# Silu gates of sequence groups 2 to 4: computed during the first group's scan and reloaded from device memory

## The chip, the cores and the metric

One Trainium2 chip, one of its cores. The metric is the device time of one execution in microseconds (us), median over runs. The profile is of one further execution. The engines are PE (matrix products, with its weight loads shown as PEld), DVE (vector), ACT (activation functions), POOL (general) and SP, which here only issues DMAs.

## The reference, cut to what matters

There are 32 sequences of 256 tokens and 256 channels. A state-space block runs first, then two attention and feed-forward layers. The change touches the first block only:

```python
xr, gate = jnp.split(x @ W_in.T, 2, axis=-1)          # 512 + 512 channels
xr = xr + t_emb[:, None, :]
xc = silu(causal_conv4(xr))                            # 4 taps per channel
xn = layernorm(xc)
# Bm, Cm, dt from xn;  Ad, Bd from dt, Bm
h  = clip(h * Ad + Bd * xn_t, -10, 10)                 # one step per token, in order
y  = Cm . h  + D * xn
out = (y * silu(gate)) @ W_out.T                       # 512 -> 256 channels
# then two layers: local attention, feed-forward
```

The gate half of `x @ W_in.T` needs only the input `x`. It does not depend on the scan, and it is used only after a step's `y` is known.

## The kernel before

**Groups, chunks and slots.** The sequences are worked in four groups of eight (`GB = 8`, groups g = 0 to 3 in the code, 1 to 4 in words). A group's scan has 256 steps, one per token for its eight sequences at once, in eight chunks of 32 (`CH`, `NCH`). `group_scan(g)` writes an agenda: a dictionary from slot to the calls to be made there, filled by `at(slot, function, ...)`. One slot is one scan step, `s0` is the slot of a chunk's first step. `scan_slots` walks the agendas of all groups in order of slots. A scheduler then fixes each engine's order, near to this one; each engine runs its own list strictly in that order, and so does each DMA queue.

**Two stages.** The scan of group 1 has no attention beside it: slots run up to 274 (`S + DRAIN`) before the first attention product. I call it the first stage. After it, attention and feed-forward of group g run interleaved with the scan of group g + 1: 16 pairs of sequence and layer for each group, while the scan makes 8 chunks. Attention of group 4 runs with no scan beside it (the last stage).

**One step** (`step`, L716): DVE makes the new state `h` of 128 x 512 from the old one and a row `xrep`. The row comes from device memory by one SP DMA (`load_rows`, six slots ahead, six buffers) and is scaled on ACT (`scale_row`, L706). In the first stage two rows of every eight are made on PE instead (`spread_rows`, tile `bx`, L693). There are eight buffers for `h`; PE reads four steps of `h` at a time into `y` (`read_out`, L728), one product for each of four blocks of 32 array columns.

**Projection in the first stage.** For group 1, `project` (L399, tile `ps_in`) makes the four convolution channel blocks and the four gate blocks of each chunk from a loaded slice of x (`load_x`, tile `xg`). Beside that, units `u` make ahead the convolution half of groups 2 to 4: `ahead_load` (x slice `xa`, by SP), `ahead_project` (four matrix products 128x256, tile `ps_a`, L426), `ahead_copy` (one ACT copy of 128x512, L437) and `ahead_put` (one SP DMA of 256 KB to device memory). There are 48 units, two for each of 24 chunks, one at every 5.33 slots from slot -30 on. `load_projected` brings them back.

**The gate in groups 2 to 4.** At each chunk `load_x` brings the x slice again (two SP DMAs of 128 KB at slot s0 + 6), `project` makes the four gate blocks at slots s0 + 13 to 18 (eight matrix products; the profile shows each as two records), `gate_th` copies each block in another order to `sg` (ACT, helper `reorder`, L371) and takes a Tanh (ACT, L768), and `gate_out` makes twice the Silu from them (DVE, L773). The factor of two is taken out of `w_out_sb`, halved once by `halve` (POOL, L331). In group 1 `gate_th` uses Silu at once, and `copy_y` (L819) puts the factor of two back. `out_gate` (L799) multiplies by `sg`, 9 slots into the next chunk for the second half; `sg` has one buffer.

Of the kernel before, what the change touches and what calls it, by code (L numbers as in the profile page):

```python
# [10 lines left out]
FP = mybir.dt.float32  # L11
BF = mybir.dt.bfloat16
I32 = mybir.dt.int32
AF = mybir.ActivationFunctionType
ALU = mybir.AluOpType
# [4 lines left out]
P = 128  # L20
# [4 lines left out]
NC_ = DI // P  # L25
NS = 16
GB = 8
CH = 32
NCH = S // CH
# [44 lines left out]
def kernel(  # L74
# [29 lines left out]
    nc = tc.nc  # L104
    B = xT.shape[2]
    L = wqkv.shape[1]
    NG = B // GB
# [55 lines left out]
    for j in range(NJ):  # L163
# [18 lines left out]
        out=mask_t[:, 0:W], in_=mask_t[:, 0:W], compare_op=ALU.is_ge, fill=MASKED_LOW,  # L182
# [39 lines left out]
    def program(ctx, exact):  # L222
# [14 lines left out]
        def constants(at):  # L237
# [86 lines left out]
                ):  # L324
                    nc.scalar.dma_start(out=t, in_=src)

            def halve():


                tc.keep_in_program_order(  # L330
                    nc.gpsimd.tensor_scalar_mul(w_out_sb, w_out_sb, 0.5)  # L331
                )

            def load_tables():

                tab, sc = work("swp", "tab", 3), work("swp", "qk_sc", 3)
# [24 lines left out]
            at(-14, sums_w)  # L361
            at(-19, decay_rate)
            at(-16, load_later)
            at(14, halve)
            at(30, load_tables)
            for n in range(2 * L):
                at(50 + 6 * n, tables, n // L, n % L)
# [1 line left out]
        def reorder(out, ps, func):  # L369

            nc.scalar.activation(  # L371
                out.rearrange("p (q i b) -> p b i q", q=NQ, b=GB),
                ps.rearrange("p (b i q) -> p b i q", q=NQ, b=GB),
                func,
            )

        def group_scan(g):
# [8 lines left out]
            alone = g == 0  # L386
# [5 lines left out]
            def at(s, what, *args):  # L392
                agendas[-1].setdefault(s, []).append(partial(what, *args))
# [14 lines left out]


            def ahead_load(u):  # L410
                if u % 2 == 0:
                    gg, c = 1 + u // 2 // NCH, u // 2 % NCH
                    t = ap_.tile([P, KM, GB, CH], FP, tag="rot", name="xa", bufs=4)
                    for k in range(KM):
                        nc.sync.dma_start(
                            out=t[:, k],
                            in_=xT[:, k, gg * GB : (gg + 1) * GB, c * CH : (c + 1) * CH],
                        )
                    state["xa", u // 2] = t

            def ahead_project(u):
                ps = bank(ps_w, "w", "ps_a").rearrange("p (r n) -> p r n", r=2)
                for r in range(2):
                    ch = 2 * (u % 2) + r
                    for k in range(KM):
                        nc.tensor.matmul(  # L426
                            ps[:, r],
                            w_in_sb[:, k, ch * P : (ch + 1) * P],
                            state["xa", u // 2][:, k],
                            start=(k == 0),  # L430
                            stop=(k == KM - 1),
                        )
                state["pa", u] = ps

            def ahead_copy(u):
                t = aw.tile([P, 2, GB * CH], FP, tag="pT", name="xs_a", bufs=6)
                nc.scalar.copy(t, state.pop(("pa", u)))  # L437
                state["ta", u] = t

            def ahead_put(u):  # L440
# [3 lines left out]

            def load_projected(c, i):
                t = sp.tile([P, 2, GB * CH], FP, tag="xg", name="xp", bufs=2)
                nc.sync.dma_start(out=t, in_=projected[((g - 1) * NCH + c) * 2 + i])
                for r in range(2):
                    ck[c]["ps", 2 * i + r] = t[:, r]


            def load_x(c):
                xg = sp.tile([P, KM, GB, CH], FP, tag="xg", name="xg", bufs=2)
# [306 lines left out]
            def gate_th(c, ch):  # L760
                if ch == 0:
                    ck[c]["sg"] = sp.tile([P, NC_, GB * CH], FP, tag="sg", name="sg")
                sg = ck[c]["sg"][:, ch]
                reorder(sg, ck[c].pop(("ps", NC_ + ch)), AF.Silu if alone else AF.Copy)
                if alone:
                    return
                th = sp.tile([P, GB * CH], FP, tag="th", name="th_g", bufs=2)
                nc.scalar.activation(th, sg, AF.Tanh, scale=0.5)  # L768
                ck[c]["th_g", ch] = th

            def gate_out(c, ch):
                sg = ck[c]["sg"][:, ch]
                nc.vector.scalar_tensor_tensor(  # L773
                    sg, ck[c].pop(("th_g", ch)), 1.0, sg, ALU.add, ALU.mult
                )

            def gated(c, hb):

# [38 lines left out]
            def copy_y(c, d):  # L817
                yo = sp.tile([P, GB, CH], FP, tag="yo", name="yo", bufs=2)
                nc.scalar.activation(  # L819
                    yo.rearrange("p b (i q) -> p q i b", q=NQ),  # L820
                    ck[c].pop(("po", d))[:, 0 : GB * CH].rearrange(
                        "p (q i b) -> p q i b", q=NQ, b=GB
                    ),
                    AF.Copy,
                    scale=2.0 if alone else 1.0,
                )
                ck[c]["yo", d] = yo

# [27 lines left out]
            for c in range(NCH):  # L856
                s0 = c * CH
                for hb in range(CH // TB):
                    s = s0 + hb * TB
                    for i in range(NI):  # L860
                        at(s + 4 * i + 5, read_out, c, hb, i)
                    at(s + 21, gated, c, hb)
                    at(s + 25, out_gate, c, hb)
                    at(s + 11, skip, c, hb)
                for ch in range(NC_):
                    at(s0 - 38 + 2 * ch, conv_in, c, ch)
                    at(s0 - 37 + 2 * ch, conv_taps, c, ch)
                    at(s0 - 36 + 2 * ch, conv_th, c, ch)
                    if not alone:
                        at(s0 - 35 + 2 * ch, conv_out, c, ch)  # L870
                for ch, s in enumerate((13, 16, 17, 18)):
                    at(s0 + s + 2, gate_th, c, ch)
                    if not alone:
                        at(s0 + s + 4, gate_out, c, ch)
                at(s0 - 25, raw_copy, c)
                at(s0 - 24, raw_turn, c)
                for j in range(NJ):
                    s = s0 - 26 + 4 * j
                    at(s + 2, norm_stats, c, j)
                    at(s + 5, norm_shift, c, j)  # L880
                    at(s + 5, norm_apply, c, j)
                    at(s + 6, norm_affine, c, j)
                    at(s + 9, norm_out, c, j)
                at(s0 - 11, length, c)
                at(s0 - 9, figures, c)
                at(s0 - 7, figures_in, c)
                at(s0 - 6, decay_th, c)
                at(s0 - 5, decays, c)
                at(s0 - 4, put_c, c, 0)
                at(s0 + 4, put_c, c, 1)  # L890
                for d in range(KM):
                    at(s0 + 45 + 2 * d, copy_y, c, d)
                    at(s0 + 46 + 2 * d, put_y, c, d)
            agendas.append({})
            for c in range(NCH):
                s0 = c * CH
                at(s0 - 43 if alone else s0 + 6, load_x, c)
                if alone:
                    for ch in range(NC_):
                        at(s0 - 40 + 2 * ch, project, c, ch)  # L900
                else:
                    for i in range(2):
                        at(s0 - 44 + 2 * i, load_projected, c, i)
                for ch, s in enumerate((13, 16, 17, 18)):
                    at(s0 + s, project, c, NC_ + ch)
                at(s0 - 27, raw_sums, c)
                for j in range(NJ):
                    at(s0 - 26 + 4 * j, norm_turn, c, j)
                at(s0 - 8, figures_out, c)
                for t in range(CH):  # L910
                    if not by_tensor(t):
                        at(s0 + t - 6, load_rows, c, t)
                    if by_tensor(t) and t % XR == 0:
                        at(s0 + t - 4, spread_rows, c, t)
                    at(s0 + t - 2, scale_row, c, t)
                for hb in range(CH // TB):
                    s = s0 + hb * TB
                    at(s - 9 if alone else s + 7, load_skip, c, hb)
                    at(s + 23, out_turn, c)
                for d in range(KM):  # L920
                    at(s0 + 43 + 2 * d, project_y, c, d)

            if alone:
                n = (NG - 1) * NCH * 2
                for u in range(n):
                    s = -30 + u * (NCH * CH) // n
                    at(s - 5, ahead_load, u)
                    at(s, ahead_project, u)
                    at(s + 2, ahead_copy, u)
                    at(s + 4, ahead_put, u)  # L930
# [731 lines left out]
```

## Time and profile before

| What | us |
|---|---|
| median of three runs | 3590.94 |
| lowest, highest of these | 3585.17, 3603.19 |
| the profiled execution's own time | 3582.75 |
| its span (first to last instruction) | 3581.0 |

| Engine | busy us | share of the span |
|---|---|---|
| PE | 3446.0 | 96% |
| PEld | 2253.9 | 63% |
| DVE | 2667.3 | 74% |
| ACT | 1998.7 | 56% |
| POOL | 1892.2 | 53% |

Busy time is the time covered by an engine's records. PE's records overlap and their ends are modelled, so PE is busy also where it could have taken more; what a product really takes is seen better in the time from one start to the next in a dense stretch. "x" counts records. Idle time is put down to what released the engine. The span holds the first stage (to about 460 us), the interleaved stage (to about 2800 us), and the last stage.

### The profile page before, as it was taken

Reading aid. Unit: us, or ns where it says so; the run is one execution under the profiler, and the core shown is the slowest. Engines: PE = TensorE matmul, PEld = TensorE weight load, DVE = VectorE, ACT = ScalarE, POOL = GpSimd, SP = SyncE. Lnnn points to the kernel's source line nnn. Section 1 sums busy time; section 2 is a strip of 40 time slices with the busy share of each in tenths; the row PEclk is TensorE's granted clock in tenths of the full one; section 3 lists DMA queues with packets and bytes.
Section 4 is the critical chain, followed back from the end, with each engine's and each line's share of the span. In section 5 each row is a group of like instructions: output and inputs, shape, how many; then the busy total and the mean of one; then the engine's idle time right before and its main releaser. Section 6 shows DMA issues by size and latency. Waiting matters only on the chain.

```text
span 3581.0 us, 57673 instructions
## 1 busy us (share of the span) xinstructions
PE 3446.0 (96%) x20220; PEld 2253.9 (63%) x20220; DVE 2667.3 (74%) x5049; ACT 1998.7 (56%) x3599; POOL 1892.2 (53%) x1842
## 2 busy tenths in 40 slices
PE   7999989999999999999999999999999999999999
PEld 4555335666656666666666666666666677777777
DVE  5888889888788777888787778888877555555553
ACT  4666656656555665566566655655666444434442
POOL 4433477645556555655565556555544454544551
PEclk9999999999999999999999999999999999999999
DMA  7887665445354545444454555534454112011101
GB/s 207 219 221 213 198 174 149 120 117 143 109 144 125 149 141 148 130 118 127 118 142 125 138 149 140 143 106 131 114 141 122 54 50 61 13 30 38 33 27 37
DMA packets 468767, 435.68 MB, mean 122 GB/s; under 512 B 228723, under 2 KB 308084, under 8 KB 468340
## 3 DMA queue, kind: packets, MB, share of 16 engines
q1 hardware_dynamic: 384018, 419.88, 42.0%
q10 hardware_dynamic: 84450, 12.01, 2.0%
q8 instruction: 163, 2.67, 0.3%
q14 instruction: 136, 1.11, 0.1%
HBM read 383.54 MB, written 46.66 MB: 120 GB/s over the span
## 4 chain that ended last, share of the span: by engine, by line
PE 61%; DVE 19%; DMA 7%; POOL 6%; ACT 4%; issue 3%; SPq 0%; ACTq 0%; DVEq 0%; POOLq 0%
PE ps_qkv L989 13%; PE pa L1375 13%; DVE h L716 7%; PE po_f L1402 7%; DMA xrep<-xnd 5%; PE ps_wo L1039 5%; PE y L728 4%; PE ov L1271 4%; PE sc L1215 3%; PE ps_out L808 3%; PE ps_in L399 2%; PE tr_qk L1028 2%; PE rs L1252 2%; ACT xrep L706 2%; DVE acc L489 2%
## 5 line engine op out<-in xcount | busy, mean ns | idle before, releaser
L716 DVE CUSTOM_DVE_ANT_0 h<-h,xrep,lim 128x512 f32<-128x512 f32 x1024 | 961.0, 938 | 228.9 <-ACT xrep L706 196.6
L706 ACT ACTIVATE xrep<-xrep,beta 128x512 f32<-128x512 f32 x960 | 672.3, 718 | 341.4 <-DMA xrep<-xnd 219.8
L989 PE MATMUL ps_qkv<-qkv,res 128*128 128x512 f32 x1536 | 713.5, 601 | 17.9 <-DVE rinv L1260 8.4
L1375 PE MATMUL pa<-hT,w 128*128 128x256 f32 (+1 forms) x2816 | 675.1, 382 | 11.3 <-DVE zT L799 10.7
L1375 PEld LDWEIGHTS pa<-hT,w 128*128 128x128 f32 (+1 forms) x2816 | 516.9, 188 | 152.9 <-issue 35.4
L1013 POOL TENSOR_TENSOR rot<-rot,swp 128x512 f32<-128x512 f32 x256 | 339.9, 1328 | 475.3 <-DVE swp L1010 423.5
L1021 POOL TENSOR_TENSOR rn<-ss,neg_half 128x8 f32<-128x8 f32 x256 | 466.8, 1823 | 18.4 <-DVE ss L1019 7.8
L989 PEld LDWEIGHTS ps_qkv<-qkv,res 128*128 128x128 f32 x1536 | 282.2, 191 | 301.6 <-issue 241.4
L728 PE MATMUL y<-h,ly 128*32 128x512 f32 x2048 | 348.9, 609 | 16.9 <-DVE h L716 13.9
L1327 POOL TENSOR_TENSOR rstd<-ve,neg_half 128x2 f32<-128x2 f32 x64 | 46.9, 733 | 527.6 <-DVE ve L1325 511.3
L1393 DVE SCALAR_TENSOR_TENSOR ag<-pa,b_sb,ag 128x256 f32<-128x256 f32 x320 | 151.6, 474 | 222.4 <-ACT ag L1386 222.3
L1402 PE MATMUL po_f<-ag,w 128*128 128x256 f32 x1280 | 309.0, 389 | 5.9 <-DVE fo L1413 3.8
L1022 POOL TENSOR_TENSOR rot<-rot,rn 128x512 f32<-128x512 f32 x256 | 289.4, 1130 | 20.0
L1402 PEld LDWEIGHTS po_f<-ag,w 128*128 128x128 f32 x1280 | 236.8, 191 | 71.3 <-issue 12.0
L1386 ACT ACTIVATE ag<-pa,b_sb 128x256 f32<-128x256 f32 x320 | 150.2, 469 | 233.1 <-PE pa L1375 232.1
L1002 ACT ACTIVATE sq<-ps_qkv 128x512 f32<-128x512 f32 x256 | 150.8, 595 | 185.1 <-PE ps_qkv L989 119.4
L1039 PE MATMUL ps_wo<-oT,wo 128*128 128x256 f32 x1024 | 231.7, 379 | 0.5 <-DVE ag L1393 0.5
L489 DVE SCALAR_TENSOR_TENSOR acc<-xr,wc_sb,acc 128x256 f32<-128x256 f32 x384 | 195.1, 531 | 47.7 <-POOL acc L478 47.2
L1005 DVE TENSOR_TENSOR rot<-ps_qkv,rc_sb 128x512 f32<-128x512 f32 x256 | 174.8, 683 | 65.6 <-ACT sq L1002 65.0
L1039 PEld LDWEIGHTS ps_wo<-oT,wo 128*128 128x128 f32 x1024 | 194.4, 190 | 28.1 <-DVE ag L1393 0.9
L1227 ACT ACTIVATE pT<-sc 128x512 f32<-128x512 f32 x384 | 202.3, 603 | 7.6 <-PE sc L1215 5.8
L1271 PE MATMUL ov<-pT,v_sb 128*64 128x256 f32 (+1 forms) x2048 | 183.7, 330 | 19.4 <-DVE ag L1393 19.3
(160 smaller groups left out, 5482.8 us busy)
## 6 DMA issues: line engine op xcount, KB each, us to landing
xrep<-xnd SPq DMA_DIRECT2D x960, 256.0 KB
rb<-inv SPq DMA_DIRECT2D x128, 256.0 KB
xnd<-xn SPq DMA_DIRECT2D x64, 256.0 KB
qkv<-in_wqkv_dram SPq DMA_DIRECT2D x24, 512.0 KB
ahead<-xs_a SPq DMA_DIRECT2D x48, 256.0 KB
xp<-ahead SPq DMA_DIRECT2D x48, 256.0 KB
xd<-xnd SPq DMA_DIRECT2D x192, 64.0 KB
w<-in_w_dram SPq DMA_DIRECT2D x80, 128.0 KB
```

The source lines that it names most:

```text
L489: nc.vector.scalar_tensor_tensor(acc, xr[:, :, k : k + CH], wc_sb[:, ch, k : k + 1], acc, ALU.mult, ALU.add,)
L706: scaled = nc.scalar.activation(bx, ck[c].pop(("bx", t), bx), AF.Copy, scale=ck[c]["beta"][:, t : t + 1])
L716: nc.vector._custom_dve(TENSOR_ADD_SAT, out=h_new, in0=state["h"], in1=bx, s0=ck[c]["lim"][:, 0, t : t + 1], s1=ck[c]["lim"][:, 1, t : t + 1],
L728: nc.tensor.matmul(ck[c]["y", hb][32 * q : 32 * q + 32, :], ly[hb % 2][:, 32 * t : 32 * t + 32], ck[c].pop(("h", hb * TB + t)), start=(i = ...
L989: nc.tensor.matmul(ps, res[b][:, k, t0 : t0 + W], wt["qkv", a][:, k], start=(k == 0), stop=(k == KM - 1),)
L1013: nc.gpsimd.tensor_add(rot, rot, swp)
L1021: nc.gpsimd.tensor_tensor(rn, ss, neg_half, ALU.pow)
L1022: nc.gpsimd.tensor_mul(rot, rot, bc(rn, 2, DH))
L1039: nc.tensor.matmul(po[:, d], wt["wo", 0][:, c, d * P : (d + 1) * P], oT[:, c, :], start=(c == 0), stop=(c == NC_ - 1),)
L1271: nc.tensor.matmul(ov[r * DH : (r + 1) * DH, i, kw * W :], self.qkv[b][2][:, kw, h * DH : (h + 1) * DH], self.p.pop((b, kw, i0 + i, r)), s ...
L1375: nc.tensor.matmul(dst[x], wt["w1", m][:, k, x], self.h[:, k], start=(k == 0), stop=(k == KM - 1),)
L1402: nc.tensor.matmul(self.po[:, d], wt["w2", 0][:, m, d * P : (d + 1) * P], self.ag[m], start=(m == 0), stop=(m == len(MCH) - 1),)
```

## The change

The units of the first stage now make all eight channel blocks of a chunk, not four: 96 units, four for each chunk, on one x slice each as before. Units 0 and 1 of a chunk are copied, units 2 and 3 (the gate) get two ACT instructions with Silu, in the order that `out_gate` reads. Each unit's result is put to device memory. The units start at slot -14 and not -30, and stand 2.875 slots apart. In groups 2 to 4, `load_x`, `project`, the Tanh and `gate_out` are gone; `load_gates` brings a chunk's four gate blocks back with two SP DMAs of 256 KB at slot s0 + 15. With no doubled gate left, `halve` and the scale in `copy_y` go.

```diff
-            def halve():
-                tc.keep_in_program_order(
-                    nc.gpsimd.tensor_scalar_mul(w_out_sb, w_out_sb, 0.5)
-                )
...
             def ahead_load(u):
-                if u % 2 == 0:
-                    gg, c = 1 + u // 2 // NCH, u // 2 % NCH
+                if u % 4 == 0:
+                    gg, c = 1 + u // 4 // NCH, u // 4 % NCH
...
             def ahead_project(u):
-                    ch = 2 * (u % 2) + r
+                    ch = 2 * (u % 4) + r
...
             def ahead_copy(u):
                 t = aw.tile([P, 2, GB * CH], FP, tag="pT", name="xs_a", bufs=6)
-                nc.scalar.copy(t, state.pop(("pa", u)))
+                ps = state.pop(("pa", u))
+                if u % 4 < 2:
+                    nc.scalar.copy(t, ps)
+                else:
+                    for r in range(2):
+                        reorder(t[:, r], ps[:, r], AF.Silu)
...
+            def load_gates(c):
+                sg = ck[c]["sg"] = sp.tile([P, NC_, GB * CH], FP, tag="sg", name="sg")
+                for i in range(2):
+                    nc.sync.dma_start(
+                        out=sg[:, 2 * i : 2 * i + 2],
+                        in_=projected[((g - 1) * NCH + c) * 4 + 2 + i],
+                    )
...
-                reorder(sg, ck[c].pop(("ps", NC_ + ch)), AF.Silu if alone else AF.Copy)
-                if alone:
-                    return
-                th = sp.tile([P, GB * CH], FP, tag="th", name="th_g", bufs=2)
-                nc.scalar.activation(th, sg, AF.Tanh, scale=0.5)
-                ck[c]["th_g", ch] = th
-
-            def gate_out(c, ch):
-                sg = ck[c]["sg"][:, ch]
-                nc.vector.scalar_tensor_tensor(
-                    sg, ck[c].pop(("th_g", ch)), 1.0, sg, ALU.add, ALU.mult
-                )
+                reorder(ck[c]["sg"][:, ch], ck[c].pop(("ps", NC_ + ch)), AF.Silu)
...
-                at(s0 - 43 if alone else s0 + 6, load_x, c)
                 if alone:
+                    at(s0 - 43, load_x, c)
                     for ch in range(NC_):
                         at(s0 - 40 + 2 * ch, project, c, ch)
+                    for ch, s in enumerate((13, 16, 17, 18)):
+                        at(s0 + s, project, c, NC_ + ch)
                 else:
                     for i in range(2):
                         at(s0 - 44 + 2 * i, load_projected, c, i)
-                for ch, s in enumerate((13, 16, 17, 18)):
-                    at(s0 + s, project, c, NC_ + ch)
+                    at(s0 + 15, load_gates, c)
...
-                n = (NG - 1) * NCH * 2
+                n = (NG - 1) * NCH * 4
                 for u in range(n):
-                    s = -30 + u * (NCH * CH) // n
+                    s = -14 + u * 276 // n
                     at(s - 5, ahead_load, u)
                     at(s, ahead_project, u)
```

More of the change, by code (lines that the diff above doesn't have):

```diff
@@ L363, in constants @@
             at(-16, load_later)
-            at(14, halve)
             at(30, load_tables)
@@ L418, in ahead_load @@
                         )
-                    state["xa", u // 2] = t
+                    state["xa", u // 4] = t
             def ahead_project(u):
@@ L428, in ahead_project @@
                             w_in_sb[:, k, ch * P : (ch + 1) * P],
-                            state["xa", u // 2][:, k],
+                            state["xa", u // 4][:, k],
                             start=(k == 0),
@@ L446, in load_projected @@
                 t = sp.tile([P, 2, GB * CH], FP, tag="xg", name="xp", bufs=2)
-                nc.sync.dma_start(out=t, in_=projected[((g - 1) * NCH + c) * 2 + i])
+                nc.sync.dma_start(out=t, in_=projected[((g - 1) * NCH + c) * 4 + i])
                 for r in range(2):
                     ck[c]["ps", 2 * i + r] = t[:, r]
+            def load_gates(c):
[5 more added lines that the diff above has]
+                    )
             def load_x(c):
@@ L762, in gate_th @@
                     ck[c]["sg"] = sp.tile([P, NC_, GB * CH], FP, tag="sg", name="sg")
-                sg = ck[c]["sg"][:, ch]
-                reorder(sg, ck[c].pop(("ps", NC_ + ch)), AF.Silu if alone else AF.Copy)
-                if alone:
-                    return
-                th = sp.tile([P, GB * CH], FP, tag="th", name="th_g", bufs=2)
-                nc.scalar.activation(th, sg, AF.Tanh, scale=0.5)
-                ck[c]["th_g", ch] = th
-            def gate_out(c, ch):
-                sg = ck[c]["sg"][:, ch]
-                nc.vector.scalar_tensor_tensor(
-                    sg, ck[c].pop(("th_g", ch)), 1.0, sg, ALU.add, ALU.mult
-                )
+                reorder(ck[c]["sg"][:, ch], ck[c].pop(("ps", NC_ + ch)), AF.Silu)
             def gated(c, hb):
@@ L824, in copy_y @@
                     AF.Copy,
-                    scale=2.0 if alone else 1.0,
                 )
@@ L870, in group_scan @@
                         at(s0 - 35 + 2 * ch, conv_out, c, ch)
-                for ch, s in enumerate((13, 16, 17, 18)):
-                    at(s0 + s + 2, gate_th, c, ch)
-                    if not alone:
-                        at(s0 + s + 4, gate_out, c, ch)
+                if alone:
+                    for ch, s in enumerate((13, 16, 17, 18)):
+                        at(s0 + s + 2, gate_th, c, ch)
                 at(s0 - 25, raw_copy, c)
@@ L896, in group_scan @@
                 s0 = c * CH
-                at(s0 - 43 if alone else s0 + 6, load_x, c)
                 if alone:
+                    at(s0 - 43, load_x, c)
                     for ch in range(NC_):
                         at(s0 - 40 + 2 * ch, project, c, ch)
+                    for ch, s in enumerate((13, 16, 17, 18)):
+                        at(s0 + s, project, c, NC_ + ch)
                 else:
@@ L903, in group_scan @@
                         at(s0 - 44 + 2 * i, load_projected, c, i)
-                for ch, s in enumerate((13, 16, 17, 18)):
-                    at(s0 + s, project, c, NC_ + ch)
+                    at(s0 + 15, load_gates, c)
                 at(s0 - 27, raw_sums, c)
```

## The prediction

> **What bounds the kernel now.** I first read the busy times by stage: where PE could take more, moved products are free, and where it can't, they cost their length. Columns: window, its length, then busy us of PE, PEld, DVE, ACT and POOL (records), granted PE clock, DMA share, GB/s.
>
> ```profile
> 100.00:340.00 240.00, 227.50 (x1003) 121.84 (x1002) 211.28 (x366) 158.45 (x290) 95.64 (x126) 0.96 0.81 219
> 385.00:437.00 52.00, 46.15 (x142) 14.27 (x142) 45.85 (x89) 31.40 (x56) 23.53 (x30) 1.00 0.65 176
> 1000.00:2500.00 1500.00, 1453.63 (x9025) 963.51 (x9024) 1205.73 (x2307) 899.74 (x1639) 878.06 (x833) 1.00 0.49 134
> 2950.00:3450.00 500.00, 500.00 (x2942) 361.08 (x2941) 272.45 (x539) 213.07 (x362) 239.81 (x199) 1.00 0.13 35
> ```
>
> The rows are the first stage with the ahead units, the first stage after the last unit, the interleaved stage and the last stage. In the interleaved stage PE stands still for 46 of 1500 us (3%), while DVE, the next, is at 80%: PE is the bound, and a product less there is time won. In the first stage PE looks 95% busy too, but the second row shows 89% with half the rate of records. So there the figure stretches, and I look at what stretches: the steps and the product `y` in the same two windows (first pair DVE's steps, L716; second pair PE and PEld of `y`, L728).
>
> ```profile
> 100.00:340.00 240.00, 151.70 (x161) 0.96 0.81 219
> 385.00:437.00 52.00, 29.45 (x35) 1.00 0.65 176
> ```
>
> ```profile
> 100.00:340.00 240.00, 61.57 (x307) 9.43 (x306) 0.96 0.81 219
> 385.00:437.00 52.00, 29.62 (x70) 4.03 (x70) 1.00 0.65 176
> ```
>
> Steps come at 240 / 161 = 1.49 us with the units and 52 / 35 = 1.49 us without: the 48 units cost the first stage nothing today, and a chunk of 32 steps takes 47.7 us either way. `y` is what gives: 0.42 us a record when each step is read as it comes, 0.20 us when PE is late and several steps are ready. The chain of waits of 100 to 380 us says what does set that pace: DVE's step 23.7%, the row's DMA 23.4%, against 3.9% for the units' products (`ps_a`). Last, the timeline of PE in dense stretches, where the next start tells the true cost (start, covered us, what).
>
> ```profile
> 206.76 1.89 PE L426 MATMUL ps_a<-xa,w_in_sb 128*128 128x256 f32 x8
> 208.58 1.35 PE L728 MATMUL y<-h,ly 128*32 128x512 f32 x6
> ...
> 216.33 1.07 PE L728 MATMUL y<-h,ly 128*32 128x512 f32 x8
> 217.32 1.99 PE L808 MATMUL ps_out<-zT,w_out_sb 128*128 128x256 f32 x8
> 219.15 1.89 PE L399 MATMUL ps_in<-xg,w_in_sb 128*128 128x256 f32 x8
> 220.97 2.22 PE L728 MATMUL y<-h,ly 128*32 128x512 f32 x8
> ```
>
> ```profile
> 1527.40 1.03 PE L399 MATMUL ps_in<-xg,w_in_sb 128*128 128x256 f32 x4
> 1528.27 1.89 PE L1375 MATMUL pa<-hT,w 128*128 128x256 f32 x8
> ```
>
> A unit of eight records costs 1.82 us (206.76 to 208.58), eight records of `y` at best 0.99 us, and one gate block of four records in the interleaved stage 0.87 us.
>
> **Removed from the interleaved stage.** 24 chunks x 4 blocks x 0.87 us = 83.5 us of PE (384 of L399's 640 records come after 437 us). They stand in PE's order between attention's products, with no idle time ahead of them, so nearly all of it is on the path. ACT loses 96 copies of 0.654 us and 96 Tanh of 0.416 us (103 us), DVE 96 products of 0.459 us (44 us); both lie beside PE and I count them at nothing, though they may shorten some of PE's 3% of waits. What could be late next is DVE, at 1205.73 - 26.66 (L773's part) of 1500 - 53: 81%, still covered. The bounds of this part: 83.5 us if PE stays the only bound, and half of that, 42 us, if waits for DVE and POOL grow into half of the freed time. I take 83.5, since the last stage shows PE without a gap when less lies beside it.
>
> **Added to the interleaved stage.** Per chunk two SP DMAs of 256 KB (`load_gates`) in place of two of 128 KB (x slices). All DMAs together took 42.0% of 16 engines for 419.88 MB, so 256 KB are about 0.94 us of all sixteen (an estimate from that row): 0.9 us more in a chunk of 102 us (471 steps in 1500 us), at a DMA share of 0.49. Covered. The added wait: the load waits until `sg` is free, which the second `out_gate` (L799) of the chunk before tells, at slot s0 + 9. It stands at slot s0 + 15 on SP, and behind it stand the row loads, for which ACT and then DVE's steps wait. But the row load next to it needs the buffer of step 15, so SP stands there anyway until that step, six slots after `out_gate`. The cost is nothing; if `out_gate` came more than six slots late, each slot further would hold the rows. The gate is used ten slots later, far over a landing of 4 to 6 us (what the rows take in the chain).
>
> **Added to the first stage.** 48 units more, and a new spacing: 32 / 2.875 = 11.1 units in a chunk instead of 6. PE's least work in a chunk, from dense rows: `ps_in` 4 x 1.82 = 7.3; `y` 8 x 0.99 = 7.9; `bx` 4 x 1.06 = 4.2; `ps_raw` 2.0; the transposes `tp_x` and `tz` 1.9; `ps_out` 2 x 1.93 = 3.9; `ps_st` 0.6; units 6 x 1.82 = 10.9. That is 38.7 us of 47.7. With 11.1 units it is 38.7 + 5.1 x 1.82 = 48.0 us. So the slack in `y` and in PE's 5.2% of idle time (12.5 of 240 us) is used up exactly, and PE becomes the bound of this stage as well. The bounds: nothing, if PE packs as densely as it can (48.0 against 47.7). If its idle share stays at 5.2%, 48.0 / 0.948 = 50.6 us, 2.9 us more in each of 276 / 32 = 8.6 chunks: 25 us. If also `y` stays at its 61.57 / 5.03 = 12.2 us in a chunk, 52.3 / 0.948 = 55.2 us: 64 us. I take 25 us: PE that is late makes `y` dense by itself, while the waits that make its idle time (a row of x, `bx`) do not go away.
>
> The other engines of this stage: ACT gets 5.6 x 2 x 0.654 = 7.3 us in a chunk (price of L371), from 66% to some 80%; 5.1 puts more are 4.8 us of DMA by the price above, from 0.81 to about 0.91 of the old chunk, 0.86 of the longer one. Neither becomes the bound alone, but each lengthens waits, which is in the bounds above. Each put waits for two Silu on ACT, and behind it on SP stand row loads; ACT's pair is done two slots before it by the agenda.
>
> Before the first step, the new start of the units takes four x-slice DMAs off SP ahead of the second chunk's x. The chain of waits holds SP's issues of that line at 8 to 14 us (1.28, 0.86, 2.54 and 0.75 us); between nothing and 5 us, I take 2 us less. `halve` (2.8 us of POOL) and the scale in `copy_y` were beside other work: nothing.
>
> **Sum.** -83.5 + 25 - 2 = -60 us. Against the profiled execution's own 3582.75 us (span 3581.0 and 1.75 us around it) this gives 3523 us. The median of the runs lies 8.2 us above that execution; I add half of it: 3527 us.
>
> [...] PEld is 51% busy in the first stage and 72% in the last, where PE never stands still. [...]
>
> The granted clock is 0.96 in the first window and 1.00 in the interleaved and last ones, where PE is denser. [...]
>
> **Rivals.**
> - *All hidden.* The first stage stays at 47.7 us a chunk: -83.5 - 2 = -86 us, 3501 us. For it: today's units are hidden whole, and the least work is 48.0 us. Against it: no other engine's order is free of waits, and PE would have to be perfect.
> - *The freed time isn't taken.* In the interleaved stage the scan's own waits set the pace: DVE waits for ACT's rows there for 122 us in 1500. Half is won: -42 + 25 - 2 = -19 us, 3568 us. Against it: PE's 3% of idle time.
> - *The first stage jams* (slower). A late unit holds the head of ACT's queue, the put behind it holds SP, row loads are late, steps come singly and `y` loses its density: half way between 7.9 and 64 x 0.42 = 27.1 us, so 9.6 us more: (48.0 + 9.6) / 0.948 = 60.8 us a chunk, +112 us, in all +26 us, 3613 us. It decides from 9.9 us a chunk on (85 / 8.6). For it: ACT already waits for `ps_a` at 10 of the 48 copies. Against it: a late PE finds several steps ready, so the loop damps itself.
>
> That the change does not do what it says is excluded: in the built order PE's products are as many as before, 192 of them moved from `ps_in` to `ps_a`, and all stand ahead of attention's first.
>
> **How the numbers follow.** Chances: forecast 0.56, all hidden 0.20, freed time not taken 0.14, jam 0.10. The range leaves out the jam and the outer ends: from 3495 us (all hidden, a little off the start) to 3575 us (half taken, with some spread). A measurement of this kernel can tell about 0.5%, 18 us, from no change. Faster by more: the first two and half of the third less a little, 0.80; within: 0.11; slower by more: 0.09.
>
> **What would show it.** In the profile after, chunks of the first stage of about 50.6 us (1.58 us a step) with `y` near 0.13 to 0.15 us a record; the interleaved stage about 3.5 us shorter for each chunk, with PE's idle share still near 3%; no waits of SP's row loads behind the gate loads. The forecast is wrong if the first stage grows past 55 us a chunk, if PE's idle share in the interleaved stage doubles, or if DVE's wait for rows rises there.

## The result and the profile after

The changed kernel takes 3634.38 us (median of four runs, 3629.39 to 3637.63) against 3588.06 us before: ratio 1.012, 95% interval 1.0088 to 1.0152. It is slower by 46 us, where 60 us less were forecast. The profiled execution took 3635.66 us, 53 us more than the one of before. In the two traces the first step of group 2's scan comes at 510 us after and at 437 us before. So the first stage lost 73 us, and everything behind it won only 20 us, not 83.5.

The rows of the first and the last stage after, with the same columns as the first rows of the prediction (window, length, busy us of PE, PEld, DVE, ACT, POOL, clock, DMA share, GB/s):

```profile
105.00:395.00 290.00, 270.31 (x1235) 161.71 (x1235) 198.71 (x366) 184.37 (x346) 95.28 (x126) 0.96 0.74 202
...
2975.00:3560.00 585.00, 585.00 (x3440) 423.45 (x3441) 320.02 (x637) 248.68 (x424) 285.44 (x236) 1.00 0.14 36
```

In the first row nothing looks full: PE has 93% (95% before), DVE fell from 88% to 69%, the DMA share from 0.81 to 0.74. Yet steps are slower. In the last row PE's records leave no gap, as in the prediction's row of the last stage; no run changed the work there. DVE's steps in the first of these two windows, and below them `y` (PE, PEld) in the same one:

```profile
105.00:395.00 290.00, 139.54 (x161) 0.96 0.74 202
```

```profile
105.00:395.00 290.00, 58.36 (x328) 8.54 (x328) 0.96 0.74 202
```

161 steps in 290 us are 1.80 us a step or 57.6 us a chunk, 9.9 more than before. `y` costs 0.18 us a record, 11.6 us a chunk, against 12.2 before: it did not become dense. The waits of the first stage, first before (100 to 400 us), then after (105 to 470 us); columns are who waits for whom, total us, times, longest (the two windows hold 200 and 205 steps):

```profile
ACT xrep L706 <- DMA xrep<-xnd: 63.5, 58, 4.2
DVE h L716 <- ACT xrep L706: 8.2, 10, 2.8
```

```profile
ACT xrep L710 <- DMA xrep<-xnd: 87.5, 75, 6.6
DVE h L720 <- ACT xrep L710: 49.6, 25, 6.1
```

The step itself waits for its row six times as long as before. Behind the first stage the later windows say where little came back: the scans of groups 2, 3 and 4 with what follows, before and then after.

```profile
437.00:1172.00 735.00, 693.58 (x4107) 428.92 (x4106) 617.85 (x1152) 440.25 (x808) 428.23 (x416) 0.98 0.50 136
1172.00:1993.00 821.00, 793.38 (x4923) 526.97 (x4920) 657.75 (x1250) 491.24 (x894) 477.30 (x453) 1.00 0.48 132
1993.00:3581.00 1588.00, 1564.08 (x9505) 1090.73 (x9503) 1034.63 (x1990) 802.92 (x1417) 805.94 (x703) 1.00 0.31 85
```

```profile
510.00:1255.00 745.00, 672.52 (x3963) 408.54 (x3966) 592.26 (x1105) 414.57 (x746) 419.01 (x406) 0.96 0.49 138
1255.00:2060.00 805.00, 774.74 (x4819) 505.98 (x4812) 646.51 (x1217) 463.42 (x829) 474.58 (x451) 0.99 0.48 137
2060.00:3634.00 1574.00, 1543.76 (x9381) 1068.84 (x9379) 1023.55 (x1957) 774.84 (x1352) 803.93 (x703) 1.00 0.31 87
```

Group 2's stretch is 10 us longer with less work on every engine: PE stands still for 72 us of it and not 41, and its granted clock fell from 0.98 to 0.96. The other two are shorter by 16 and 14 us; 27.8 us each was the price of their gate products. Over all three PE's busy time fell by 60 us and its idle time rose by 40.

### The profile page after: what moved, and what is told of

Same layout as the page of the kernel before. It is cut to its first block, busy times and chain, and to the rows that moved or that the text cites. A ratio compares the mean times of both kernels' runs of the same rounds, so it can differ in the third digit from the quotient of the medians.

```text
span 3633.9 us, 57619 instructions
## 1 busy us (share of the span) xinstructions
PE 3447.6 (95%) x20220; PEld 2259.9 (62%) x20220; DVE 2614.7 (72%) x4953; ACT 1960.7 (54%) x3503; POOL 1876.4 (52%) x1841
## 4 chain that ended last, share of the span: by engine, by line
PE 54%; DVE 17%; POOL 10%; DMA 10%; ACT 5%; issue 4%; SPq 1%; ACTq 0%; DVEq 0%; POOLq 0%
PE ps_qkv L980 12%; PE pa L1366 12%; PE po_f L1393 7%; DMA xrep<-xnd 7%; DVE h L720 7%; PE ps_wo L1030 4%; PE y L732 3%; PE ov L1262 3%; PE sc L1206 3%; POOL rn L1012 2%; PE tr_qk L1019 2%; DVE acc L493 2%; ACT xrep L710 2%; PE rs L1243 2%; PE ps_a L418 1%
## 5 line engine op out<-in xcount | busy, mean ns | idle before, releaser
L980 PE MATMUL ps_qkv<-qkv,res 128*128 128x512 f32 x1536 | 727.4, 610 | 34.6 <-ACT oT L1269 9.7
L732 PE MATMUL y<-h,ly 128*32 128x512 f32 x2048 | 323.5, 616 | 24.8 <-DVE h L720 19.5
L493 DVE SCALAR_TENSOR_TENSOR acc<-xr,wc_sb,acc 128x256 f32<-128x256 f32 x384 | 183.9, 498 | 44.1 <-POOL acc L482 43.7
L1218 ACT ACTIVATE pT<-sc 128x512 f32<-128x512 f32 x384 | 201.9, 601 | 12.7 <-PE sc L1206 10.6
L418 PE MATMUL ps_a<-xa,w_in_sb 128*128 128x256 f32 x768 | 193.5, 397 | 8.3 <-ACT xs_a L431 5.6
```

The costliest lines, as they stand in the source:

```text
L418: nc.tensor.matmul(ps[:, r], w_in_sb[:, k, ch * P : (ch + 1) * P], state["xa", u // 4][:, k], start=(k == 0), stop=(k == KM - 1),)
L493: nc.vector.scalar_tensor_tensor(acc, xr[:, :, k : k + CH], wc_sb[:, ch, k : k + 1], acc, ALU.mult, ALU.add,)
L732: nc.tensor.matmul(ck[c]["y", hb][32 * q : 32 * q + 32, :], ly[hb % 2][:, 32 * t : 32 * t + 32], ck[c].pop(("h", hb * TB + t)), start=(i = ...
L980: nc.tensor.matmul(ps, res[b][:, k, t0 : t0 + W], wt["qkv", a][:, k], start=(k == 0), stop=(k == KM - 1),)
```

## The experiments

Two theories for the first stage. **Queue**: a put waits on SP for two Silu, row loads stand behind it, ACT waits for rows with the units' copies behind them, and so on in a circle. **PE**: the added products cost their full length, because the rest of PE's order does not pack. Two theories for the rest: PE's work is not worth its length there, or the freed time goes into a new order of the other engines.

### The two halves alone

`e1_gain` is the changed kernel with the 48 units of before: the gates' work is out of the later groups and nothing is added to the first stage (the gate loads read the convolution half):

```diff
-                        in_=projected[((g - 1) * NCH + c) * 4 + 2 + i],
+                        in_=projected[((g - 1) * NCH + c) * 2 + i],
...
-                n = (NG - 1) * NCH * 4
+                n = (NG - 1) * NCH * 2
                 for u in range(n):
-                    s = -14 + u * 276 // n
+                    s = -30 + u * (NCH * CH) // n
```

> The removal alone: the 48 units of the first stage as in the kernel before, no gate is projected for groups 2 to 4 and load_gates reads the convolution half in its place (the gates' projection and Silu are left out). First stage as before (first step of group 2 at 437 us). If PE is the only bound of the interleaved stage, as the prediction has it, 83.5 us are won and some more at the table's other ends: about 3500 us. If the later stages give back only what the changed kernel showed behind its first stage (20 us), or the freed time goes into waits, about 3545 to 3570 us.

Measured: 3565.66 us, ratio 0.9937 (0.9915 to 0.9959). First step of group 2 at 438 us, as before.

`e2_cost` is the kernel before with the 96 units of the changed one (its gates in device memory are not read):

> The addition alone: 96 units in the first stage with Silu and puts, while the interleaved stage still projects its own gates as before. If the first stage's loss is all from the added units, the first step of group 2 comes at 510 us as in the changed kernel (437 before) and the time is the kernel before plus 73 us, 3660 us. By the prediction's 25 us it would be 3613 us.

Measured: 3667.87 us, ratio 1.0215 (1.0189 to 1.024); first step of group 2 at 512 us. The two halves add up: 77 - 25 = 52 us, 46 were measured together. Each half misses by itself.

### The first stage: SP's queue, ACT, the ring of rows, or PE

The trace of the changed kernel seems to speak for the queue. Here is SP at 249 to 263 us (start, us, queue, line, what), at the row loads of steps 118 to 130:

```profile
249.12 3.58 SPq L689 DMA_DIRECT2D xrep<-xnd  x4
252.81 0.66 SPq L749 DMA_DIRECT2D xq<-xnd  x1
255.80 0.31 SPq L439 DMA_DIRECT2D ahead<-xs_a  x1
...
258.49 0.32 SPq L439 DMA_DIRECT2D ahead<-xs_a  x1
...
262.91 3.34 SPq L689 DMA_DIRECT2D xrep<-xnd  x5
```

After 252.81 SP stands until a Silu pair ends at 255.8, and no row is asked for until 262.91. Of this gap of 10.2 us, 2.3 us are the wait of that put; most of the rest are the loads of other tiles that stand between (`xq`, `xa`, `xg`; left out in the lines shown). ACT too holds its order: it stood 4.38 us for a row until 208.26, with a unit's Silu behind it (208.89) whose products had ended by 204.40. `e3_actput` takes the puts off SP:

```diff
-                nc.sync.dma_start(out=d, in_=state.pop(("ta", u)))
+                nc.scalar.dma_start(out=d, in_=state.pop(("ta", u)))
```

> The changed kernel with the units' puts issued from ACT's queue, right behind the ACT instruction that makes the tile, so that SP's row loads no longer stand behind a put that waits for ACT. Queue theory (SP is held by puts, rows come late, ACT waits for rows with the units' copies behind it): the first stage falls back to about 51 to 53 us a chunk, first step of group 2 at 455 to 470 us, time 3580 to 3595 us. PE theory (PE's added work sets the pace): 58 us a chunk stays, 510 us, 3634 us. ACT pays 96 issues of some 0.35 us in either case.

(The 0.35 us is an estimate: one issue on ACT's queue, `ys` at 251.16, covers 0.37 us in the trace after, and the median put on SP 0.34 us.)

`e4_noput` leaves the puts of the gate units out:

```diff
             def ahead_put(u):
+                if u % 4 >= 2:
+                    state.pop(("ta", u))
+                    return
```

> The changed kernel without the puts of the gate units (load_gates reads the convolution half instead, so the gates in groups 2 to 4 are wrong values): PE's products and ACT's Silu stay, 48 puts of 256 KB and their waits on SP go. Queue theory: first stage about 52 us a chunk, time 3575 to 3590 us, near the run with puts from ACT. Volume theory (the bytes of the puts lengthen the rows' landing): clearly below that run, as only here the bytes go. PE theory: still 58 us a chunk, 3634 us.

`e5_copy` gives a gate unit one copy (`if u % 4 < 2:` becomes `if True:`):

> The changed kernel with one ACT copy for a gate unit in place of two Silu (the gates' Silu and reordering are left out): ACT is relieved by some 0.75 us a unit, 4.2 us in a chunk of the first stage; PE's products and the puts stay. PE theory: chunks stay at 57 to 58 us, time about 3630 us. ACT theory (rows wait behind the Silu pairs in ACT's queue): chunks near 53 to 54 us, time about 3600 us.

`e6_halfpe` halves its products:

```diff
-                    for k in range(KM):
+                    nk = KM if u % 4 < 2 else 1
+                    for k in range(nk):
...
-                            stop=(k == KM - 1),
+                            stop=(k == nk - 1),
```

> The changed kernel with two products instead of four in each gate unit (half of the gate's sum is left out): PE is relieved by 0.91 us a unit, 5.1 us in a chunk of the first stage; ACT's Silu and the puts stay. PE theory: each us of PE work counts once PE is full, chunks fall by 5 us or more to 52 to 53 us, time about 3590 us. ACT theory or ring theory: chunks stay near 57 us, 3630 us.

`e7_rows7` has seven row buffers (`bufs=7`, rows at `s0 + t - 7`, attention's `swp` buffers 2 instead of 3):

> The changed kernel with seven row buffers and row loads seven slots ahead instead of six; the memory is taken from a buffer of attention, so only the chunks of the first stage are compared. Ring theory (six buffers, and each takes longer from load to step, since units stand between on SP, ACT and PE): chunks fall toward 57.9 x 6/7 = 50 us. PE theory: they stay at 57 to 58 us.

Measured, the chunk from the steps in the window of 105 to 395 us, and the whole stage from its first step to the first step of group 2:

| Run | steps | chunk us | stage us | time us | ratio (interval) |
|---|---|---|---|---|---|
| changed kernel | 161 | 57.6 | 456 | 3634.38 | 1.012 (1.0088 to 1.0152) |
| e3_actput | 170 | 54.6 | 442 | 3625.74 | 1.0096 (1.0075 to 1.0116) |
| e4_noput | 166 | 55.9 | 456 | 3632.91 | 1.0117 (1.0092 to 1.0143) |
| e5_copy | 164 | 56.6 | 451 | 3632.93 | 1.012 (1.0074 to 1.0166) |
| e6_halfpe | 177 | 52.4 | 420 | 3605.55 | 1.0042 (1.0029 to 1.0056) |
| e7_rows7 | 162 | 57.3 | 454 | 3702.36 | 1.0313 (1.0283 to 1.0343), attention has fewer buffers |

How much of this is scatter can be seen in the kernel before and the eight runs that leave its first stage as it was: theirs takes 386 to 394 us, so 1 us a chunk means nothing.

The queue theory falls but for a part: without the puts' waits on SP 3 of the 9.9 us go, and the whole time moves by 9 us, with intervals that overlap. In `e3_actput` the same rows stand still at the same place, for 9.4 us, with no put on SP:

```profile
251.07 1.49 SPq L689 DMA_DIRECT2D xrep<-xnd  x2
255.07 2.63 SPq L749 DMA_DIRECT2D xq<-xnd  x4
...
261.97 3.70 SPq L689 DMA_DIRECT2D xrep<-xnd  x5
```

Volume, ACT's Silu and the ring of rows are worth 0.3 to 1.7 us a chunk in the window and 0 to 5 us over the stage, little or no more than the scatter. PE's half is worth 5.2 us a chunk for 5.1 us of product time, one for one, and 36 us over the stage. A striking wait in a trace had shown where the lateness is felt, not what makes it. One reservation: these runs have the scheduler's own order of instructions. In the first stage of `e5_copy` and `e7_rows7` the traces show almost that of the changed kernel, but in `e6_halfpe` some 190 of DVE's 677 instructions there stand elsewhere. What that is worth wasn't measured.

The rows of the units (`ps_a`: PE, PEld) close the account, before, after and in `e6_halfpe`:

```profile
100.00:340.00 240.00, 59.97 (x240) 45.52 (x240) 0.96 0.81 219
```

```profile
105.00:395.00 290.00, 112.39 (x447) 85.19 (x447) 0.96 0.74 202
```

```profile
105.00:395.00 290.00, 93.89 (x366) 68.60 (x366) 0.96 0.81 221
```

A unit's eight records cover 2.00, 2.01 and 2.05 us. In a chunk the units' products take 11.9 of 47.7 us before, 22.3 of 57.6 us after and 17.0 of 52.4 us with the half products. They leave 35.8, 35.3 and 35.4 us: everything else on PE, its idle time included, takes the same in all three and gives nothing more, so between 6 and 11.1 units a chunk a further unit cost its length (10.4 us more of products, 9.9 us more of chunk). Two chunks stand outside this account. The first one took 50.8 us after, with 12.5 units, and 53.0 us before, with 7. And the last one before took 47.2 us with no unit in it, so there the steps keep their pace for another reason; which, no run shows.

### The rest: gate loads, PE's work, and order

`e8_noload` is `e1_gain` with the gates loaded once:

```diff
             def load_gates(c):
+                if "sg" in projected:
+                    ck[c]["sg"] = projected["sg"]
+                    return
...
+                projected["sg"] = sg
```

> The run with the removal alone, further without the gate loads but the first chunk's (all later chunks use its values): 46 SP DMAs of 256 KB less. If the gate loads, or SP's wait in them, eat part of the interleaved stage's gain, this run is faster than the removal alone (3566 us) by up to 40 us. If PE's own waits and clock eat it, it stays within 6 us of 3566 us.

Measured: 3566.74 us, ratio 0.9914 (0.9883 to 0.9945), against 0.9937 (0.9915 to 0.9959) with the loads. The gate loads cost nothing that these runs can tell, as predicted.

`e9_half` makes one of the two products of each gate block of groups 2 to 4 in the kernel before:

> The kernel before, with one product instead of two in each gate block of groups 2 to 4 (half of the gate's sum is left out); ACT, DVE, DMA and the number of instructions but PE's as before. If PE's work counts in full, half of 83.5 us is won: 42 us, 3548 us. If PE's work counts as in the run with the removal alone (25 of 83.5), some 12 us, 3578 us.

`e10_nope` makes none of them:

```diff
+                ps = ck[c].pop(("ps", NC_ + ch)) if alone else w_in_sb[:, 0, 0 : GB * CH]
...
-                for ch, s in enumerate((13, 16, 17, 18)):
-                    at(s0 + s, project, c, NC_ + ch)
+                if alone:
+                    for ch, s in enumerate((13, 16, 17, 18)):
+                        at(s0 + s, project, c, NC_ + ch)
```

> The kernel before without any gate product in groups 2 to 4 (the copies read a constant tile, the gates are wrong values); ACT's copies and Tanh, DVE's products, the x slices stay. If PE's work alone decides: the whole 83.5 us, 3507 us. If what the run with the removal alone showed is all that PE's work is worth, 3566 us. If in that run the missing ACT and DVE work did harm by another order, this one is clearly faster than 3566 us.

`e11_nogateout` keeps the products and drops Tanh and `gate_out` (`gate_th` returns after the copy):

> The kernel before without Tanh and gate_out in groups 2 to 4 (the gate's Silu is left out); PE's gate products and the reordering copies stay. ACT is relieved by 40 us and DVE by 44 us over the interleaved stage. By the prediction (both lie beside PE): no change, 3588 us. If DVE or ACT shares the bound: up to 40 us less. If their missing changes the order for the worse: slower than 3588 us.

Measured: `e9_half` 3590.24 us (0.9985, 0.997 to 1.0), `e10_nope` 3587.67 us (0.9983, 0.9966 to 1.0001), `e11_nogateout` 3652.83 us (1.0163, 1.0146 to 1.018). Taking work away gives nothing or makes the kernel 57 us slower. (The kernel before, measured beside each of these three, took 3595.71 us; beside the pinned runs below, 3588.81 us.) In the traces each of these edits leaves PE's order nearly untouched (2 to 12 of some 20000 records stand elsewhere), but the scheduler gives DVE, ACT and POOL another one: of DVE's 5050 instructions 1000 to 2000 stand elsewhere. So three runs hold the order. A list in the kernel chains all instructions of ACT, DVE, POOL and SP in the order that the kernel before has:

```diff
+            for name, perm in order.items():
...
+                for a, b in zip(perm, perm[1:]):
+                    tc.add_manual_dep(
+                        mine[b], mine[a].name,
...
```

`p2_nope` is `e10_nope` so pinned, `p5_nogateout` is `e11_nogateout` so pinned, `p4_double` is the kernel before, pinned, with each gate product of groups 2 to 4 made twice. The kernel before with the list and no other edit was not run; that the list by itself costs little is seen only in `p5_nogateout`, 7 us below the kernel before.

> The run without gate products in groups 2 to 4 (3588 us with its own order), with the order of ACT, DVE, POOL and SP pinned to that of the kernel before; the gates are wrong values. Order theory (PE's work is worth its length, but each edit makes the scheduler choose another order of the other engines, which takes it back): near 3588 - 83.5 = 3505 us, at least below 3550 us. Second-bound theory (a chain over the other engines is as long as PE's work, so PE's relief buys nothing): stays at 3580 to 3590 us.

> The kernel before with each gate product of groups 2 to 4 made twice (gates doubled, wrong values), order of ACT, DVE, POOL and SP pinned: 83.5 us more PE work, nothing else. Both theories have PE full at 97%, so added work costs its length: 3588 + 83 = 3670 us. If PE has hidden room (its 97% is stretched), under 3630 us.

> The run without Tanh and gate_out in groups 2 to 4 (3653 us with its own order; the gate's Silu is left out), with the order of ACT, DVE, POOL and SP pinned to that of the kernel before. Order theory: the 57 us of loss are all from the order, so this run comes back to 3588 us or below. If the loss is from something else (buffers free at another time), it stays near 3650 us.

Measured:

| Work against the kernel before | own order | order of before |
|---|---|---|
| no gate products (-83.5 us of PE) | 3587.67 us, 0.9983 (0.9966 to 1.0001) | 3550.88 us, 0.9893 (0.9877 to 0.991) |
| no Tanh, no gate_out | 3652.83 us, 1.0163 (1.0146 to 1.018) | 3582.01 us, 0.9981 (0.9971 to 0.9991) |
| gate products twice (+83.5 us of PE) | not run | 3655.24 us, 1.0191 (1.0174 to 1.0208) |

Same work, another order: 30 us in the first line and 64 us in the second, each run taken against the kernel before of its own session (37 and 71 us between the medians as they stand). In the traces 67 us of the second line lie behind the first step of group 2, 22 of them in group 3's scan. There they can be seen on PE, in the groups of products. First `e11_nogateout` with its own order, then pinned (columns: records, busy us, mean ns, idle us before them and what ended it; the list moves the line numbers):

```profile
L1399 PE MATMUL po_f<-ag,w 128*128 128x256 f32 x320 | 89.2, 433 | 24.3 <-DVE fo L1410 14.7 <-DVE res L1410 9.6
```

```profile
L1708 PE MATMUL po_f<-ag,w 128*128 128x256 f32 x320 | 79.1, 395 | 3.2 <-DVE fo L1719 3.2
```

It is the same product on the same place of PE's order; DVE's result that it waits for stands up to 17 places later in DVE's list. With the order held, DVE's and ACT's relief is worth 0.2%, as good as beside the path. PE's work is worth 66 us when 83.5 are added and 38 us when 83.5 are taken away: added work finds PE full, and when work goes, waits for other engines take more than half of the freed time. The scan of group 2 with no gate products, with its own order and pinned, then the two later rows of the pinned run:

```profile
446.00:1194.00 748.00, 680.65 (x3975) 409.98 (x3976) 615.86 (x1155) 436.79 (x809) 431.84 (x418) 0.96 0.51 135
```

```profile
435.00:1165.00 730.00, 671.13 (x3984) 406.10 (x3986) 620.85 (x1153) 438.80 (x807) 425.22 (x416) 0.97 0.50 138
1165.00:1973.00 808.00, 767.52 (x4794) 500.66 (x4787) 659.98 (x1251) 489.93 (x895) 477.27 (x453) 1.00 0.48 134
1973.00:3549.00 1576.00, 1538.59 (x9373) 1066.20 (x9371) 1036.78 (x1990) 800.18 (x1417) 806.36 (x703) 1.00 0.31 85
```

Pinned group 2's scan is 18 us shorter, but PE still stands for 59 of 730 us, where it stood for 41 of 735 with the gate products in place. Over the three pinned rows PE's busy time is 74 us below the kernel before and its idle time 44 us above it. In group 2 this idle time is spread over many products, with DVE as the engine most waited for (`y` for a step 12.7 us and 7.5 before, `po_f` for the residual 4.8 us and 2.1 before), and the clock is 0.97 there, 0.98 before.

## Why the prediction was wrong, step by step

- **"PE is the bound: a product less there is time won" (-83.5 us)** failed. The removal alone gave 25 us. PE is full upward (66 of 83.5 us added count, 80%) and not downward: 38 of 83.5 us, 45%, with the order held; with the scheduler's own order 8 of 83.5 us and, for half of the products, 5 of 42 us, both with intervals that reach to no change. The view misread was the idle share: 3% said that PE was busy then, and nothing on how far behind the next limit was. The lower end of 42 us was about the worth at a fixed order; that the edit also buys a new order on three engines was in no term, and it took back some 30 us where PE's products alone were removed.
- **PE's least work in a chunk (38.7 us, 48.0 with the new units; +25 us)** failed. The dense rows show what PE did where nothing was missing; the rest of its order, idle time included, took 35.8 us beside 11.9 us of units before and 35.3 us after, where the sum had 27.8. That late PE makes `y` dense was wrong: `y` took 12.2 us a chunk before and 11.6 us after, not 7.9. The measured loss is 9.9 us on average in the seven chunks behind the first, which itself got 2 us shorter: 67 us, above the upper end of 64 us.
- **The start (-2 us)** went the other way: the first step comes at 54 us and not 48. Over the runs with 48 units it came at 48 to 52 us, with 96 at 53 to 58. Six of the 73 us are here; their cause was not looked for.
- **The jam** came near the right chunk (60.8 us) by the wrong mechanism: off SP, the puts give back 3 us, and `y` took no more than before. The circle that it describes can be seen in the waits, and is mostly an effect.
- **The rival "freed time isn't taken"** came closest for the later stages (42 us, 20 measured), but it had a first stage of 25 us. The result needed its low gain and the jam's long chunks together, and no line of the forecast had both.
- **Costed at nothing and not seen to cost**: the gate loads and their wait (1 us between `e1_gain` and `e8_noload`), ACT's and DVE's relief with the order held (7 us), and ACT's Silu in the first stage (1.0 us a chunk, within the scatter).
- **Weight loads and the clock.** Weight loads covered 51% of the first stage before and 56% after (161.71 / 290), against 72% in the last stage; the added units were not free all the same, so here a low share of weight loads did not show room. The clock of the first stage stayed at 0.96, with PE busy 95% before and 93% after by its records. In group 2's scan PE's idle time rose from 41 to 72 us, and the clock fell from 0.98 to 0.96, which would be about 15 us of 745 if the scan's time went with the clock (an estimate from these two clocks). Over nine traces of that scan (the kernel before and after, `e1_gain`, `e2_cost`, `e10_nope`, `e11_nogateout` and the three pinned runs) the clock is 0.98 to 0.99 with 37 to 48 us of idle time, 0.97 with 53 to 59 and 0.96 with 67 to 72; which of the two makes the other, no run shows. Between stages it did not go with PE's busy share: in the kernel before it was 1.00 at 89% (385 to 437 us) and 0.96 at 95% (100 to 340 us).

What stays open: why `e1_gain` gains 17 us more than `e10_nope`, each against its own kernel before, though both leave the same products out (ACT's and DVE's work, the x slices and the order all differ; the removal alone with the order of before was not tried); which single chain is the limit behind PE; and what the first stage would be with its order held. Of the runs that make the gates ahead, none came below the kernel before: in the first stage a gate unit costs more (67 us for 48) than it returns (25 us).

## What to carry to other kernels

PE, busy 96% of the span, told here what added work costs (66 of 83.5 us) but not what removed work returns (38 of 83.5 us); make a run that takes the work away before planning to move it. Room found under a load may be used up: 48 units went with steps of 1.49 us, the same as without units, and 48 more cost 67 us. Test with half and with double before adding as much again. And where a scheduler orders the queues anew at each edit, hold the order in one run, since here the order alone was worth 30 and 64 us, as much as the whole edit.

## What the runs showed that was not expected

A kernel with less work on ACT and DVE, and otherwise the same, was 57 us slower (3652.83 us) and, with the same work in the old order, 7 us faster (3582.01 us): the order of the queues was worth almost 2% with no instruction added. And the row loads' stop of 10 us, which looked like the work of a put on SP, was 9.4 us long without any put there; taking all puts off SP moved the whole time by 9 us.
